# A top-2 expert layer with a shared expert: every expert over every token, or 23 tiles of routed rows fetched through DRAM

## The chip, the cores and the metric

The kernel runs on one core of a Trainium2 chip. The time is the device time of one execution in microseconds. The core has a matrix engine (TensorE, PE in the profile; PEld is its weight load), a vector engine (DVE), a scalar engine (ACT), a general engine (POOL) and a queue engine (SP) that issues most DMA transfers.

## The reference

A stack of four layers works on x of 4 x 256 tokens with 256 features (1024 tokens in all), each layer an attention over a context of 1601 rows and a feed-forward part, both with a layer norm ahead and a residual sum behind. The change is in the last feed-forward part and reaches into the attention ahead of it (16 heads of 128, 4 key heads, over the same context). Cut to what matters:

```python
# E = 8 experts of width 128, top 2; a shared expert of width 512
x = x + attention_3(layernorm(x), ctx)
h = layernorm(x).reshape(1024, 256)
probs = softmax(h @ w_gate)
topk_w, topk_ids = top_k(probs, 2)
topk_w = topk_w / sum(topk_w)
combine = sum(topk_w * one_hot(topk_ids, 8))
act = silu(g) * u      for g, u = split(einsum('th,ehf->etf', h, w_gate_up))
eo = einsum('eti,eih->eth', act, w_down)
routed = einsum('te,eth->th', combine, eo)
shared = (silu(g) * u for g, u = split(h @ w_sh_gate_up)) @ w_sh_down
x = x + routed + shared
```

All numbers are f32.

## The kernel before

The tokens lie in eight tiles X[0] to X[7] of 128 tokens by 256 features; a batch b of the four is the pair X[2b], X[2b+1].

**The last feed-forward part** (`shared_moe`, L1905 to L1957) starts from a transposed norm of all tokens (`layernorm`, halves of 512 tokens). `router` (L187) makes all probabilities, `top2` the two choices, and `comb` holds one weight per token and expert. Then a loop runs over the eight experts and, last, the shared expert; inside it over the two halves. Per half of an expert it makes gate and up products for 512 tokens (L1942), `gated` (L1745, L1746) makes silu times up, and four down products (L1948) come back with 128 tokens on the partitions. Each is added to X with the expert's weight (L1955), whatever that weight is: an expert works on all 1024 tokens, also on those that did not choose it. The shared expert has four such gate and up parts per half and sums four products per tile; its sums go by `residual` (L181) and the tiles are stored (L1953). TensorE, ScalarE and VectorE are ordered here by the scheduler.

**The attention ahead of it** (`gqa`, L1001) is laid out by hand in slots. Sixteen units (batch and key head) take 16 slots each; slot t has phases "first", "early", "mid", "late", "last", "values", "pe", "post", and `at(slot, phase, f)` puts a step there. The scores of a slot go to two of three PSUM tiles (L1235); VectorE takes their maxima (L1243), ScalarE the exponentials (L1244), which also frees the tile; POOL scales them (L1284), VectorE transposes blocks (L1289), and TensorE makes the value products (L1315) and the output products (L1328), which `residual` adds to X. The engines TensorE, ScalarE, VectorE and POOL keep the written order; SP is ordered by the scheduler.

**The same routing elsewhere.** The first layer's feed-forward part already works on routed rows: `send_to_experts` (L586) ranks each token within its expert and scatters rows to the DRAM table XS (L727), and `sparse_moe` (L738) fetches tiles of 128 rows from it (L817), the first eight at fixed rows and fifteen more at rows held in registers (L805). The third layer's `capacity_moe` (L1749) scatters (L1845), fetches (L1853), stores results (L1888) and gathers them back per token (L1899). Each expert has room for 1024 rows in XS, so 2048 routed rows of eight experts need at most 8 + 15 = 23 tiles of 128.

Of the kernel before, what the change touches and what calls it, by code (L numbers as in the profile page):

```python
# [12 lines left out]
F32 = mybir.dt.float32  # L13
I32 = mybir.dt.int32
# [38 lines left out]
def kernel(ctx: ExitStack, tc: tile.TileContext, A, out: bass.AP):  # L53
# [683 lines left out]

    def sparse_moe(r, k, XS, XD, tabs):  # L738
        ET = mybir.EngineType
        NT = E + MORE  # L740
        with (
# [18 lines left out]
            for f in r["last"]:  # L760
                f()

            ps = ps_acc()
            nc.tensor.matmul(ps[:, 0:E], k["ones"], r["cum"], start=True, stop=True)
            cnt = small([P, E], "d_cnt", 1)
            nc.vector.tensor_copy(cnt, ps[:, 0:E])
            over = small([P, E, E - 1], "d_over", 1)
            nc.vector.tensor_tensor(
                over, cnt.unsqueeze(2).to_broadcast([P, E, E - 1]),
                k["step"].unsqueeze(1).to_broadcast([P, E, E - 1]), ALU.is_gt,  # L770
            )
            nc.vector.tensor_reduce(cnt, over, AX.X, ALU.add)
            upto = small([P, E], "d_upto", 1)
            t8 = small([P, E, E], "d_t8", 1)
            nc.vector.tensor_tensor(t8, k["tri8"], cnt.unsqueeze(1).to_broadcast([P, E, E]), ALU.mult)
            nc.vector.tensor_reduce(upto, t8, AX.X, ALU.add)
            oh = one.tile([P, MORE, E], F32, tag="d_oh", name="d_oh")
            g = one.tile([P, MORE, E], F32, tag="d_g", name="d_g")
            wide = [P, MORE, E]
            more = k["more"].unsqueeze(2).to_broadcast(wide)  # L780
            nc.vector.tensor_tensor(oh, more, upto.unsqueeze(1).to_broadcast(wide), ALU.is_ge)
            ex = small([P, MORE], "d_ex", 1)
            nc.vector.tensor_reduce(ex, oh, AX.X, ALU.add)
            nc.vector.tensor_tensor(
                oh, k["expert"].unsqueeze(1).to_broadcast(wide), ex.unsqueeze(2).to_broadcast(wide), ALU.is_equal
            )

            nc.vector.tensor_tensor(cnt, cnt, upto, ALU.subtract)
            nc.vector.scalar_tensor_tensor(cnt, cnt, float(P), k["first"], ALU.mult, ALU.add)
            nc.vector.scalar_tensor_tensor(  # L790
                g, more, float(P), cnt.unsqueeze(1).to_broadcast(wide), ALU.mult, ALU.add
            )
            nc.vector.tensor_tensor(g, g, oh, ALU.mult)
            row = small([P, MORE], "d_row", 1)
            nc.vector.tensor_reduce(row, g, AX.X, ALU.add)
            none = small([P, MORE], "d_none", 1)
            nc.vector.tensor_scalar(none, ex, E - 0.5, float(E * ROOM), ALU.is_gt, ALU.mult)
            nc.vector.tensor_tensor(row, row, none, ALU.add)
            nc.vector.tensor_scalar(ex, ex, E - 1.0, 4096.0, ALU.min, ALU.mult)
            ix = one.tile([P, 2, MORE], I32, tag="d_ix", name="d_ix")  # L800
            nc.vector.tensor_copy(ix[:, 0, :], row)
            nc.vector.tensor_copy(ix[:, 1, :], ex)
# [198 lines left out]
    def gqa(xT, key, tabs=None, early=None):  # L1001
# [12 lines left out]
        with (  # L1014
# [324 lines left out]

            weights(0)  # L1340
# [564 lines left out]
    def shared_moe(xT):  # L1905
        with (
            tc.tile_pool(name="l3f", bufs=2) as pool,
            tc.tile_pool(name="l3f1", bufs=1) as one,
        ):
            wg = one.tile([P, NC_, E], F32, tag="wg", name="wg")  # L1910
            nc.sync.dma_start(wg, A["l3f_wg"])
            ws = []
            for k in range(2):
                w = wslot()
                nc.sync.dma_start(w[:, 0:3072].rearrange("p (e f) -> p e f", e=4), A["l3f_w"][:, k * 4 : (k + 1) * 4, :])
                ws += [w[:, i * 768 : (i + 1) * 768] for i in range(4)]
            shw = wslot()
            nc.sync.dma_start(shw[:, 0:3072], A["l3f_sw"])
            probs = router(one, xT, wg)
            m1, m2, comb = top2(one, probs)  # L1920
            nc.vector.tensor_tensor(m1, m1, m2, ALU.add)
            nc.vector.reciprocal(m1, m1)
            nc.vector.tensor_tensor(comb, comb, bc(m1, E), ALU.mult)

            parts = []
            for e in range(E):
                gu = ws[e][:, 0:512].rearrange("p (c f) -> p c f", c=2)
                parts.append(([(gu[:, :, 0:I3], gu[:, :, I3:])], [ws[e][:, 512:768]], e))
            sgu = shw[:, 0:2048].rearrange("p (c f) -> p c f", c=2)
            parts.append((  # L1930
                [(sgu[:, :, i * P : (i + 1) * P], sgu[:, :, ISH + i * P : ISH + (i + 1) * P]) for i in range(4)],
                [shw[:, 2048 + i * D : 2048 + (i + 1) * D] for i in range(4)],
                None,
            ))
            for gus, downs, e in parts:
                for hf in range(2):
                    acts = pool.tile([P, len(gus), 512], F32, tag=f"act{len(gus)}", name="acts")
                    for i, (wgt, wup) in enumerate(gus):
                        pg, pu = ps_acc(), ps_acc()
                        for ps, wt in ((pg, wgt), (pu, wup)):  # L1940
                            for c in range(NC_):
                                nc.tensor.matmul(ps, wt[:, c, :], xT[hf][:, c, :], start=(c == 0), stop=(c == NC_ - 1))  # L1942
                        gated(pool, acts[:, i, :], pg, pu)
                    for t in range(4):
                        j = hf * 4 + t
                        ps = ps_tr()
                        for i, wd in enumerate(downs):
                            nc.tensor.matmul(  # L1948
                                ps[:, :D], acts[:, i, t * P : (t + 1) * P], wd, start=(i == 0), stop=(i == len(downs) - 1)
                            )  # L1950
                        if e is None:
                            residual(j, ps[:, :D])
                            nc.sync.dma_start(out[j * P : (j + 1) * P, :], X[j])  # L1953
                        else:
                            nc.vector.scalar_tensor_tensor(  # L1955
                                X[j], ps[:, :D], comb[:, j, e : e + 1], X[j], ALU.mult, ALU.add
                            )  # L1957
# [11 lines left out]
    with tc.tile_pool(name="sort", bufs=1) as sortp:  # L1969
        k = sort_constants(sortp)  # L1970
        with rings(0, x=0, s1=2, kv=2, tr=2, acc=2):
            r = topk_attention(lambda: send_to_experts(sortp, k, XS), KD, VD)
        with rings(0, x=0, tr=3, acc=5):
            sparse_moe(r, k, XS, XD, tabs)
# [96 lines left out]
```

## Time and profile before

| what | value |
|---|---|
| median of three runs | 3896.47 us (3893.48 to 3897.65) |
| the profiled execution | 3896.89 us, of which the span of the profile is 3895.1 us |
| TensorE busy | 3656.7 us, 94% of the span |
| VectorE, ScalarE, POOL busy | 2612.1, 1677.2, 1278.0 us |
| mean granted TensorE clock | 0.971 of full speed |

The span is the time from the first to the last instruction of the profiled execution; the time of the execution is 1.8 us longer. Instructions are named by engine, line, operation and by the tiles they write and read. A matmul of f32 data is listed as two. "Idle before" is the time in which an engine waited ahead of an instruction, with what ended the wait.

### The profile page before, as it was taken

The numbers are of one execution on the slowest core, as the hardware profiler recorded it, in microseconds if no ns is written. First come the engines' busy times: TensorE is split into PE (matmuls) and PEld (weight loads), VectorE is DVE, ScalarE is ACT, GpSimd is POOL, SyncE is SP. The second block draws the span as 40 slices with busy tenths as digits, with TensorE's granted clock in tenths as the row PEclk, the third lists the DMA queues.
The fourth block names the chain that finished last, engine by engine and source line by source line (L and its number), as shares of the span: only waits on it lengthen the run. The fifth ranks groups of instructions, "written<-read, shape, count | busy, mean of one in ns | idle before, by whom it ended". The sixth has DMA issues, their size and how long they took to land.

```text
span 3895.1 us, 62649 instructions
## 1 busy us (share of the span) xinstructions
PE 3656.7 (94%) x23428; PEld 2176.8 (56%) x23428; DVE 2612.1 (67%) x5037; ACT 1677.2 (43%) x4898; POOL 1278.0 (33%) x2046
## 2 busy tenths in 40 slices
PE   8887969999999999999899999987999999999999
PEld 4557945555555555555445454563455565555555
DVE  7884857777777777777566565436777766666653
ACT  4443635444444444454134444513344444454421
POOL 2332535444544544443300101013333333333310
PEclk9987979999999999999999999988999999999999
DMA  7326342222222221210200000033111011111010
GB/s 236 101 66 236 79 148 62 64 81 57 55 66 62 75 66 54 65 51 1 72 1 18 6 13 1 1 138 114 51 44 58 28 40 50 34 41 41 7 49 11
DMA packets 165553, 238.22 MB, mean 61 GB/s; under 512 B 20333, under 2 KB 127745, under 8 KB 161665
## 3 DMA queue, kind: packets, MB, share of 16 engines
q1 hardware_dynamic: 160401, 226.96, 18.8%
q0 software_dynamic: 4848, 7.25, 1.0%
q8 instruction: 186, 3.05, 0.3%
q14 instruction: 118, 0.97, 0.1%
HBM read 194.28 MB, written 39.88 MB: 60 GB/s over the span
## 4 chain that ended last, share of the span: by engine, by line
PE 65%; DVE 18%; POOL 7%; issue 5%; ACT 3%; DMA 2%; SPq 0%; DVEq 0%; POOLq 0%; ACTq 0%
PE acc L1315 15%; PE sc L1235 13%; PE tr L1104 5%; PE sc L1608 4%; DVE PT L1289 4%; PE sc L1562 3%; PE tr L1178 3%; PE acc L1629 3%; POOL pe L1284 3%; PE acc L877 2%; PE acc L1942 2%; PE tr L1517 2%; PE tr L1328 2%; POOL t L1151 2%; DVE ms L1243 2%
## 5 line engine op out<-in xcount | busy, mean ns | idle before, releaser
L1244 ACT ACTIVATE pe<-sc,ms 128x480 f32<-128x480 f32 (+1 forms) x1024 | 644.1, 632 | 942.1 <-DVE ms L1243 923.7
L1315 PE MATMUL acc<-PT,V 128*128 128x256 f32 (+1 forms) x3584 | 897.7, 391 | 7.7 <-ACT OT L1322 7.2
L1235 PE MATMUL sc<-KT,QT 128*32 128x480 f32 (+5 forms) x8192 | 888.0, 535 | 14.0 <-ACT pe L1244 6.2
L1284 POOL TENSOR_SCALAR pe<-pe,fac 128x480 f32<-128x480 f32 (+1 forms) x1024 | 654.9, 659 | 636.5 <-ACT pe L1244 304.9
L1315 PEld LDWEIGHTS acc<-PT,V 128*128 128x128 f32 (+1 forms) x3584 | 643.0, 190 | 350.7 <-issue 181.9
L1243 DVE TENSOR_REDUCE ms<-sc 128x1 f32<-128x480 f32 (+1 forms) x1024 | 607.9, 615 | 170.3 <-PE sc L1235 145.5
L1289 DVE STREAM_TRANSPOSE PT<-pe 128x1920 f32<-128x1920 f32 (+1 forms) x256 | 519.5, 2030 | 0.0
L122 POOL TENSOR_TENSOR rs<-rsq_t,mhalf 128x2 f32<-128x2 f32 (+2 forms) x248 | 159.9, 645 | 880.8 <-DVE rsq_t L121 821.5
L1235 PEld LDWEIGHTS sc<-KT,QT 128*32 128x32 f32 x8192 | 218.8, 109 | 408.6 <-issue 308.6
L1104 PE MATMUL tr<-w,cx 128*128 128x256 f32 (+1 forms) x1264 | 303.3, 382 | 1.3 <-ACT nk L1120 1.3
L1614 ACT ACTIVATE pt<-sc 128x1024 f32<-128x1024 f32 (+1 forms) x224 | 214.1, 960 | 201.1 <-PE sc L1608 192.8
L1568 DVE TENSOR_REDUCE mx<-sc 128x2 f32<-128x1024 f32 (+1 forms) x192 | 207.2, 1089 | 114.6 <-PE sc L1562 65.3
L1608 PE MATMUL sc<-QT,KT 32*128 32x256 f32 (+1 forms) x1664 | 235.8, 405 | 21.2 <-DVE mx L1568 14.5
L1104 PEld LDWEIGHTS tr<-w,cx 128*128 128x128 f32 (+1 forms) x1264 | 227.0, 187 | 31.6 <-ACT nk L1120 2.0
L1562 PE MATMUL sc<-KT,QT 32*128 32x512 f32 (+2 forms) x1024 | 229.1, 553 | 0.7 <-DVE mx L1568 0.6
L1244 ACT ACTIVATION_READ_ACCUMULATOR pe<-sc,ms 128x1 f32 x1024 | 199.9, 195 | 0.0
L1608 PEld LDWEIGHTS sc<-QT,KT 32*128 32x128 f32 (+1 forms) x1664 | 136.7, 183 | 79.0 <-DVE mx L1568 51.2
L122 POOL TENSOR_TENSOR rsq<-rsq_t,mhalf 128x4 f32<-128x4 f32 x64 | 64.9, 1014 | 324.4 <-DVE rsq_t L121 324.4
L1112 ACT ACTIVATE sq<-tr 128x128 f32<-128x128 f32 (+1 forms) x348 | 97.1, 279 | 170.7 <-PE tr L1104 164.2
L121 DVE TENSOR_SCALAR rsq_t<-ss 128x2 f32<-128x2 f32 (+2 forms) x248 | 46.4, 188 | 177.2 <-ACT sq L1112 139.8
L1178 PE MATMUL tr<-w,xlnT 128*128 128x512 f32 x256 | 125.1, 612 | 4.4 <-DMA w<-in_l1a_wkv 4.1
L1562 PEld LDWEIGHTS sc<-KT,QT 32*128 32x128 f32 x1024 | 84.3, 190 | 76.6 <-issue 41.8
(373 smaller groups left out, 4864.2 us busy)
## 6 DMA issues: line engine op xcount, KB each, us to landing
cx<-in_ctxT SPq DMA_DIRECT2D x144, 256.0 KB, 3.1
tab<-rope SPq DMA_DIRECT2D x112, 256.0 KB, 2.7
w<-in_l0f_w SPq DMA_DIRECT2D x8, 2048.0 KB, 14.4
ctxT<-in_ctxT SPq DMA_DIRECT2D x7, 1601.0 KB, 7.3
w<-in_l2f_w SPq DMA_DIRECT2D x8, 1088.0 KB, 18.1
w<-in_l1a_wq SPq DMA_DIRECT2D x16, 512.0 KB, 5.9
wo<-in_l1a_wo SPq DMA_DIRECT2D x16, 512.0 KB, 7.7
w<-in_l3a_wq SPq DMA_DIRECT2D x16, 512.0 KB, 5.9
```

Of the source, the lines that this page charges most:

```text
L122: nc.gpsimd.tensor_tensor(dst, t[:n, :k], mhalf[:n, :k], ALU.pow)
L1104: nc.tensor.matmul(v["ps"][:n, i, :], lhs, st["wkv"][:, c, :], start=(c == 0), stop=(c == NC_ - 1))
L1178: nc.tensor.matmul(v["ps"], xtok(xT, b * 2 + tt, c), state[u]["wq"][:, c, :], start=(c == 0), stop=(c == NC_ - 1))
L1235: nc.tensor.matmul(sc[32 * r : 32 * r + 32, 0 : lens[r]], st["QT"][:, tt, o : o + 32], st["KT"][:, r, 0 : lens[r]], start=True, stop=True,)
L1243: nc.vector.tensor_reduce(top, sc, AX.X, ALU.max, negate=True)
L1244: nc.scalar.activation(w, sc, AF.Exp, bias=top, accum_out=s)
L1284: nc.gpsimd.tensor_scalar(w, w, v["fac"][:, g * 4 + a : g * 4 + a + 1], 1.0, ALU.mult, ALU.mult)
L1289: nc.vector.transpose(state[steps[i]][:, :, g * P : (g + 1) * P].rearrange("p k (a t) -> p a k t", a=4), pes[g].rearrange("p a (k i) -> p ...
L1315: nc.tensor.matmul(v["ps"][:, 0 : 2 * P], V[:n, k, :], PT[:n, k, :], start=(k == 0), stop=(k == nch - 1))
L1562: nc.tensor.matmul(st[:, j, :n], QT[r, g, tt * P : (tt + 1) * P], KT[r, g, o : o + n], start=True, stop=True)
L1608: nc.tensor.matmul(st[:n, j, q, :], KT[r, g, o : o + n], QT[r, :], start=True, stop=True)
L1614: nc.scalar.activation(pt[:n, 2 * hp : 2 * hp + 2, :m], st[:n, :, :m], AF.Exp)
```

## The change

`shared_moe` no longer runs every expert over every token.

- `send_to_shared` makes norm, router, both choices, weights and ranks of one batch in small steps. For batches 0 to 2, `others` puts these steps into free slots of the attention, from slot 4(16b + 15) + 13 on, with four scatters of 128 rows each (two tiles, two choices) to XS, one per slot. Table constants and the shared expert's weights are made or loaded ahead of the attention.
- After the attention, `shared_moe` writes its order by hand for TensorE, ScalarE and VectorE. The first part of the shared expert's first half (`up(0, 0)`) stands ahead of the last batch's norm and routing; `up(0, 1)`, `up(0, 2)`, `up(0, 3)` and the sums `down(0)` stand between and behind its steps.
- `more_tiles` (taken out of `sparse_moe`, where its steps stay the same) finds from the counts which expert and row each of the fifteen further tiles has. A register with the row is loaded on SP for each fetch, and one with the weight's column on TensorE for each tile, tile by tile.
- Each of the 23 tiles is fetched, transposed (`turn`), multiplied with gate and up weights together (`first`), gated, transposed back (`back`), multiplied with the down weights (`second`) and stored to the DRAM table OQ.
- Then come `up(1, 0)` to `up(1, 3)`. `collect(j)` gathers two rows per token from OQ, adds them with their weights to X[j] and stores the tile: tiles 0 to 3 ahead of the sums `down(1)`, 4 to 7 behind them.

The diff, cut to its core:

```diff
-    def shared_moe(xT):
...
-            for gus, downs, e in parts:
-                for hf in range(2):
...
+        def others(at, done):
+            for b in range(B - 1):
+                t = done(b)
+                p = batch(b)
+                for i, phase, name in (
+                    (0, "early", "stats"), (0, "late", "scale"), (1, "pe", "turn"), (2, "early", "turned"),
+                    (2, "pe", "logits"), (3, "early", "exps"), (4, "late", "probs"), (5, "late", "first"),
+                    (6, "late", "second"), (7, "late", "count"), (8, "pe", "ranks"), (9, "early", "rows"),
+                ):
+                    at(t + i, phase, p[name])
+                for q in range(4):
+                    at(t + 9 + q, "late", lambda p=p, q=q: p["send"](q // 2, q % 2))
...
+            rest = up(0, 0)
+            for name in ("stats", "scale", "turn", "turned", "logits", "exps", "probs", "first", "second", "count"):
+                last[name]()
+            rest()
+            rest = up(0, 1)
+            last["ranks"]()
+            last["rows"]()
+            for q in range(4):
+                last["send"](q // 2, q % 2)
+            rest()
+            up(0, 2)()
+            ix, _, _, less = more_tiles(one, k, r["cum"], float(WIDE3))
...
+            def fetch(t):
+                x = pool.tile([P, D], F32, tag="xs", name="xs", bufs=8)
+                if t < E:
+                    nc.sync.dma_start(x, XS[t * ROOM : t * ROOM + P, 0:D])
+                else:
+                    nc.sync.dma_start(x, XS[bass.ds(register(ET.SP, 0, t - E, E * ROOM), P), 0:D])
...
+            for t in range(E):
+                fetch(t)
...
+            up(0, 3)()
+            down(0)
+
+            def turn(t):
+                v = tiles[t]
+                if t >= E:
+                    v["at"] = register(ET.PE, 1, t - E, (E - 1) * WIDE3)
+                tr = ps_tr()
+                for c in range(NC_):
+                    nc.tensor.transpose(tr[:, c * P : (c + 1) * P], v["x"][:, c * P : (c + 1) * P], ident)
+                v["xT"] = pool.tile([P, NC_, P], F32, tag="xsT", name="xsT", bufs=3)
+                nc.vector.tensor_copy(v["xT"], tr[:, 0:D].rearrange("p (c t) -> p c t", c=NC_))
...
+            def second(t):
+                v = tiles[t]
+                ps = ps_acc()
+                nc.tensor.matmul(ps[:, 0:D], v["aT"], part(t, 4 * I3, 4 * I3 + D), start=True, stop=True)
+                y = pool.tile([P, D], F32, tag="y", name="y", bufs=4)
+                nc.scalar.copy(y, ps[:, 0:D])
+                nc.sync.dma_start(OQ[t * P : (t + 1) * P, :], y)
+
+            for t in range(NT + 3):
+                for f, i in ((turn, t), (first, t - 1), (back, t - 2), (second, t - 3)):
+                    if 0 <= i < NT:
+                        f(i)
+                if E <= t + 5 < NT:
+                    fetch(t + 5)
+            for i in range(4):
+                up(1, i)()
...
+            def collect(j):
+
+                b, i = divmod(j, 2)
+                y = one.tile([P, 2, D], F32, tag=f"g{j}", name=f"g{j}")
+                for c in range(2):
+                    nc.gpsimd.indirect_dma_start(
+                        y[:, c], None, OQ[:, :], bass.IndirectOffsetOnAxis(ap=iq[:, b, c, i : i + 1], axis=0)
+                    )
+                for c in range(2):
+                    nc.vector.scalar_tensor_tensor(X[j], y[:, c], r["w"][:, b, c, i : i + 1], X[j], ALU.mult, ALU.add)
+                nc.sync.dma_start(out[j * P : (j + 1) * P, :], X[j])
+
+            for j in range(4):
+                collect(j)
+            down(1)
+            for j in range(4, NJ):
+                collect(j)
...
-    with rings(3):
-        shared_moe(layernorm())
+    with tc.tile_pool(name="sort3", bufs=1) as sortp:
+        shw = sortp.tile([P, 3072], F32, tag="shw", name="shw")
+        nc.sync.dma_start(shw, A["l3f_sw"])
+        with rings(0, sc0=1, sc1=1, sc2=1, tr=4, acc=1):
+            xT = layernorm()
+            k = sort_constants(sortp)
+            r, batch, others = send_to_shared(sortp, k, XS)
+            gqa(xT, "l3a", early=(EARLY, KD, VD), others=others)
+        with rings(0, x=0, tr=3, acc=5):
+            shared_moe(r, k, shw, batch(B - 1), XS, OQ)
```

## The prediction

> **What bounds the kernel now.** I read the page, then the chain of waits in order of time, then the windows by stage.
>
> ```profile
> span 3895.1 us, 62649 instructions
> PE 3656.7 (94%) x23428; PEld 2176.8 (56%) x23428; DVE 2612.1 (67%) x5037; ACT 1677.2 (43%) x4898; POOL 1278.0 (33%) x2046
> ```
>
> TensorE is busy throughout, so work taken from it should count. The end of the chain (start, time, engine, tile, line) is the changed stage:
>
> ```profile
> 3749.61 1.74 PE tr L1328 x8
> ...
> 3808.66 2.57 PE acc L1942 x6
> 3814.09 2.58 PE acc L1942 x6
> ...
> 3852.05 12.02 PE acc L1942 x28
> 3864.06 6.91 PE tr L1948 x32
> ```
>
> L1328 is attention's last product; it ends at 3751.4, and the stage takes 3895.1 - 3751.4 = 143.7 us. Call 3751.4 zero. An f32 product is listed as two matmuls (passes). One period of 5.43 us (3814.09 - 3808.66) is half an expert: eight passes of 512 columns and eight of 256. The last two lines give 0.43 us a pass of 512 and 0.216 us a pass of 256.
>
> The windows (length; busy PE, PEld, DVE, ACT, POOL; granted clock, DMA share, GB/s) compare the stages:
>
> ```profile
> 2700.00:2800.00 100.00, 95.25 (x649) 49.64 (x643) 71.42 (x135) 39.28 (x119) 31.36 (x51) 1.00 0.12 39
> 3500.00:3600.00 100.00, 98.35 (x658) 58.16 (x654) 66.05 (x137) 48.77 (x171) 36.94 (x60) 1.00 0.16 44
> 3755.00:3762.00 7.00, 6.92 (x32) 6.52 (x33) 1.39 (x4) 0.58 (x1) 0.00 (x0) 0.50 1.01 421
> 3800.00:3850.00 50.00, 50.00 (x149) 27.38 (x149) 23.12 (x47) 5.37 (x9) 0.00 (x0) 1.00 0.00 0
> ```
>
> The routed stage is TensorE alone at full clock; POOL and the queues are idle. Attention ahead of it has TensorE at 95 to 98% and VectorE at 66 to 71%: work moved there finds little room on TensorE.
>
> **Removed.** Routed products: 16 periods x 5.43 = 86.9 us. Norm and router between 3751.4 and 3761.6: 10.2 us, part of it at half clock.
>
> **Added on TensorE: the tile loop.** A tile costs two transposes, two products of 256 columns, a transpose and one more product. Six passes x 0.216 = 1.30; a transpose of 128 columns has a pitch of 0.11 us (the two of L855 start 0.22 us ahead of the next product), so 0.33. That is 1.63 us, and 23 tiles take 37.5 us. Beside it per tile lie VectorE 0.42 (copy, L857) + 0.29 (128x128 product, L1660) and ScalarE 0.28 + 0.28 + 0.37 (L1112, L1887's form) = 0.93, both shorter and one to two tiles behind, so hidden. Filling and draining the pipeline adds about 2.
>
> **Register loads.** Fifteen tiles load one register each on TensorE's queue and one on SP's. The old expert stage loads fifteen in one instruction (L805):
>
> ```profile
> L805 PEldq TENSOR_LOAD <-d_ix x1: 4428/4428/4428, 306.6 to 306.6; - x1
> L805 SPq TENSOR_LOAD <-d_ix x1: 1892/1892/1892, 348.8 to 348.8; - x1
> ```
>
> Divided, one is 0.13 (SP) to 0.30 us (TensorE, with weights streaming in). The Trainium skill (DMA: Bandwidth & Descriptors, "Latency and other measured facts") speaks against loading singly: it gives a floor of about 600 ns to a load, to be spread by unrolling four. By the row the fifteen cost 2 to 4.5 us of the queue, by the rule 9. Either lies behind matmuls already sent, if the queue runs ahead: a tile's last input is ready some 0.4 us into its 1.63 us, so about 0.9 us is covered. No row shows a load among running matmuls; bounds are 0 and the whole 4.43 each (52 us after cover). I take 2 us in all, nearest the divided row, and keep up to 9. The address arithmetic on TensorE's queue (46 ns each at L896) left its eight passes at 1.89 us there, so nothing. SP has a load, a fetch (0.34, L817) and a store (0.32, L1888) per tile, 0.8 to 1.3 us against 1.63: eight buffers and stores one tile late keep it off the path, unless its load took over 1 us. The gate's table load (1.28 us, ScalarE) is in both kernels and lies beside the routing.
>
> **Added: the last batch's routing.** The old expert stage has the same chain: from its last sum (290.4) to the rows (302.2) 11.8 us, in small vector steps of 0.17 every 0.21. Here the first shared product (0.5 to 3.9) delays the transposes by 1 us and one gate product sits in the chain: rows at about 13.4. Four scatters follow on POOL:
>
> ```profile
> 2574.99 0.96 POOL L1845 DMA_INDIRECT xd<-nat,ix  x1 [0.30 <-issue]
> 2576.26 0.96 POOL L1845 DMA_INDIRECT xd<-nat,ix  x1 [0.30 <-issue]
> ...
> 2578.67 3.65 SPq L1853 DMA_DIRECT2D xs<-xd  x8
> ```
>
> One each 1.27 us; SP fetches 2.4 us after the last begins. So issues at 13.5 to 17.3, fetch at 20, first tile by 22.5 (2.1 us to landing). Beside it TensorE does four shared parts (13.8), the routing's own passes (2) and the first four sums (6.9). It waits twice: about 1.1 us for the ranks, and for the fourth shared part's gate, because VectorE does the tables first: 4.1 us as at L766 to L802, then twelve more steps, 2.8 us, so the gate at 23.2 while that product ended at 18.4 and the six passes that need no gate at 19.7. That is 3.6 us idle; the remaining 26 passes end at 28.9.
>
> Does the clock fall? The rows around 3733:
>
> ```profile
> 3714.12 2.00 PE L1315 MATMUL acc<-PT,V 128*128 128x256 f32 x8
> ...
> 3733.91 3.40 PE L1315 MATMUL acc<-PT,V 128*128 128x256 f32 x8
> ```
>
> After 1.85 us without a matmul eight passes took 3.40 instead of 2.00 us, and the slow stretch lasted about 5. The Trainium skill (TensorE: Matmul & The Clock Gate, "Part 1: The HAM clock gate") asks for at least one idle window of about 3.4 us first. By the row the 1.1 us wait is nearly enough too and both together cost 3; by the rule only the long one, 1.7 at most. I take 2: loop from 30.9. The tiles have landed by then.
>
> **The end.** Loop 37.5 + 2 + 2, to 72.4. Copy 0.4 and the store's landing 1.7 (L1888), with gaps: 74.8. Then sixteen gathers on POOL, where capacity_moe's eight ran every 1.25 us and landed in 2.8 (L1899): last issued at 74.8 + 15 x 1.25 = 93.6, landed 96.4, weighted sum 0.48 each: 97. From the last sum to the end of the span the old kernel took 3895.1 - 3892.1 = 3.0: 100. TensorE's other shared half ends at 72.4 + 13.7 + 0.9 + 6.9 = 93.9, so the gathers are late next, by 3 us. The stage gains 143.7 - 100 = 43.7.
>
> **Moved into attention (three batches).** TensorE each: four transposes 0.45, eight narrow passes and four rank passes at about 0.13 = 1.6; together 2.1, x3 = 6.3 us with next to no slack (9.6 if the passes cost the 0.21 of L193 at half clock). VectorE: about 7 us each over twelve slots, in order ahead of score maxima that release TensorE's score banks; a slot of 3.6 to 4.5 us has 1.2 to 1.5 free. Nothing to 7 us a batch can show; I take 5 in all, since most steps come after the maxima. POOL: twelve scatters of 1.26 us, one a slot, each waiting for the one before; they precede L1284's scalings, whose transposes follow two slots later, so 0 (12 x 1.26 = 15 us were that slack gone). At the start thirteen table and fill instructions (2 us) stand on POOL ahead of the first rsqrt, and SP issues 1.5 MB of shared weights and the gate ahead of attention's weights (0.8 us of issue, 3.7 us at 421 GB/s); the first weights wait about 3 us for their norm now, which covers most: 1 us, at most 4. Sum 12.3. The routed weights come at the end while TensorE does shared work (3 MB, 7.5 us): covered until 22.
>
> **Sum.** -43.7 + 12.3 = -31.4. The profiled execution took 3896.9 (1.8 outside its span), the median 3896.5: 3865.
>
> **Rivals.**
> - *The moves are free* (chance 0.17): attention absorbs the vector steps, the clock stays up, loads hide. Then 5 + 1 + 2 + 2 us fall away: 3855. For it: VectorE is 29 to 34% idle there. Against: 95% busy TensorE with waits on maxima.
> - *VectorE stalls attention* (0.13): all 7 us of each batch show, 21 instead of 5: 3881. For it: ScalarE waits for maxima all through (L1244 on L1243). Against: maxima mostly have 2 us of bank slack.
> - *Slower: single register loads stop TensorE* (0.07). In the tile loop each load waits with the queue empty at the full 4.43 us; 15 x (4.43 - 0.9) = 53 less the 2 counted: 3916. Above about 3.1 us a load, the gain is gone. For it: the only TensorE load traced cost that. Against: it read fifteen values, and SP's took 1.89.
> - That the tiles are not made is excluded: their count is fixed at 23 whatever is routed, 2944 rows against 8192.
>
> **Numbers.** The forecast has 0.63. A difference under 0.2% (7.8 us) is about what a measurement here cannot tell from none. Faster: 0.61 + 0.17 + 0.08 = 0.86; same: 0.02 + 0.05 = 0.07; slower 0.07. The range reaches down to the free moves with the gathers hidden too (3) and TensorE's 6.3 in its gaps, 3846, and up to stalled attention (3881) with loads at the rule's 9 us and a start of 4, 3891.
>
> **What would show it.** Right: 1.6 us between tiles from the eighth on as before it, attention's last product 10 to 15 us later, sixteen gathers back to back at the end with TensorE done. Wrong: TensorE idle at each load; tiles waiting for fetches behind stores on SP; attention longer by over 20 us; or routing so late that the first tile waits.

## The result and the profile after

The changed kernel took 3858.86 us (median of six runs, 3857.5 to 3860.84) against 3895.88 us before (six runs beside it, 3892.45 to 3897.65). The ratio is 0.9905, 95% interval 0.9894 to 0.9915: 37 us faster. The forecast was 3865 us, with faster at 0.86; the time lies in the range and 6 us under the forecast.

The first two lines of the page after (span; busy time, share and instructions of each engine):

```profile
span 3856.3 us, 63026 instructions
PE 3603.5 (93%) x23397; PEld 2157.0 (56%) x23397; DVE 2611.3 (68%) x5142; ACT 1688.0 (44%) x4956; POOL 1310.3 (34%) x2091
```

TensorE's busy time fell by 53 us, but only 38.8 us of it came out of the span: TensorE is no longer what ends the kernel. The chain of waits says what does (start, time, engine, tile, line):

```profile
3756.44 1.74 PE tr L1335 x8
...
3758.68 3.70 PE acc L2104 x8
...
3780.45 5.89 PE tr L2113 x26
...
3819.01 0.87 PE acc L2194 x4
...
3820.64 0.87 PE acc L2194 x4
...
3825.04 1.73 PE acc L2104 x4
...
3827.94 0.99 POOL g L2230
...
3847.20 3.18 DMA g<-oq,g_ix
```

L1335 is attention's last product. The residual sum behind it starts at 3758.20, which I call zero as the prediction did for before (3751.37 there). L2104 is a shared part, L2113 the shared sums, L2194 a tile's gate and up product: 3820.64 - 3819.01 = 1.63 us a tile. From 3827.94 on the chain is gathers. The stage ends at 98.1 us from zero; before it took 143.7.

The windows (length; busy PE, PEld, DVE, ACT, POOL; granted clock, DMA share, GB/s):

```profile
2700.00:2800.00 100.00, 95.06 (x648) 48.86 (x646) 71.02 (x135) 39.79 (x122) 32.30 (x53) 1.00 0.12 39
3500.00:3600.00 100.00, 97.91 (x653) 59.82 (x645) 70.08 (x168) 47.30 (x166) 37.18 (x57) 1.00 0.17 49
3758.00:3765.00 7.00, 5.76 (x23) 3.16 (x23) 2.20 (x8) 0.58 (x1) 0.71 (x1) 1.00 0.83 314
3795.00:3820.00 25.00, 25.00 (x140) 21.11 (x139) 10.80 (x31) 12.17 (x46) 0.00 (x0) 1.00 0.42 129
```

Attention's stretches hardly changed; behind zero the clock is full where before it was half, and the tile loop fills TensorE, though each tile has a register load.

### The profile page after: what moved, and what is told of

Its sections match the earlier page's. It is cut to its first block, busy times and chain, and to the rows that moved or that the text cites. A ratio compares the mean times of both kernels' runs of the same rounds, so it can differ in the third digit from the quotient of the medians.

```text
span 3856.3 us, 63026 instructions
## 1 busy us (share of the span) xinstructions
PE 3603.5 (93%) x23397; PEld 2157.0 (56%) x23397; DVE 2611.3 (68%) x5142; ACT 1688.0 (44%) x4956; POOL 1310.3 (34%) x2091
## 4 chain that ended last, share of the span: by engine, by line
PE 64%; DVE 18%; POOL 7%; issue 5%; ACT 3%; DMA 3%; SPq 1%; POOLq 0%; DVEq 0%; ACTq 0%
PE acc L1322 15%; PE sc L1242 13%; PE tr L1111 5%; PE sc L1618 4%; DVE PT L1296 4%; PE sc L1572 3%; PE tr L1185 3%; PE acc L1639 3%; POOL pe L1291 3%; PE acc L884 2%; PE tr L1527 2%; PE tr L1335 2%; POOL t L1158 2%; DVE ms L1250 2%; ACT pe L1251 2%
## 5 line engine op out<-in xcount | busy, mean ns | idle before, releaser
L1250 DVE TENSOR_REDUCE ms<-sc 128x1 f32<-128x480 f32 (+1 forms) x1024 | 607.5, 615 | 173.3 <-PE sc L1242 147.2
```

Of the source, the lines that this page charges most:

```text
L1250: nc.vector.tensor_reduce(top, sc, AX.X, ALU.max, negate=True)
```

## The experiments

All times of the table come from one profiled execution each, the medians from all runs. "Attention" runs from the first score maximum (L1250, before L1243) of the third unit to zero. It leaves out the stages ahead, which no edit touches and which came out up to 10 us apart between executions (2771.1 us in one_load, 2781.2 in part_behind). The kernel before took 3894.8 to 3897.4 us in the median beside the groups of runs. The other columns count from zero. Before: attention 975.0 us, end 143.7.

| kernel | median us | ratio to before, 95% | attention | first tile | last gather begins | end |
|---|---|---|---|---|---|---|
| after | 3858.9 | 0.9905 (0.9894 to 0.9915) | 983.1 | 28.0 | 89.0 | 98.1 |
| again | 3861.0 | 0.9910 (0.9893 to 0.9926) | 983.1 | 28.0 | 88.7 | 97.7 |
| stats_late | 3854.9 | 0.9894 (0.9879 to 0.9909) | 980.0 | 29.6 | 90.7 | 101.6 |
| tables_late | 3860.5 | 0.9908 (0.9893 to 0.9923) | 983.2 | 25.5 | 86.5 | 97.5 |
| sums_late | 3863.6 | 0.9918 (0.9904 to 0.9931) | 983.2 | 22.2 | 84.9 | 102.4 |
| part_behind | 3871.2 | 0.9929 (0.9915 to 0.9942) | 983.2 | 34.2 | 95.2 | 106.2 |
| route_after | 3901.9 | 1.0012 (1.0003 to 1.0021) | 976.7 | 74.6 | 135.6 | 146.6 |
| one_load | 3868.4 | 0.9921 (0.9907 to 0.9934) | 987.3 | 29.7 | 90.7 | 101.6 |
| loads6 | 3866.1 | 0.9919 (0.9906 to 0.9933) | 987.3 | 29.7 | 93.7 | 104.2 |
| best | 3855.6 | 0.9893 (0.9878 to 0.9908) | 980.0 | 22.1 | 82.9 | 98.9 |
| copied | 3860.0 | 0.9907 (0.9891 to 0.9924) | 983.2 | 28.0 | 89.0 | 98.1 |
| two_late | 3854.2 | 0.9894 (0.9878 to 0.9911) | 979.9 | 25.5 | 86.5 | 95.6 |
| three | 3852.1 | 0.9884 (0.9867 to 0.9900) | 980.0 | 25.5 | 86.5 | 95.6 |

**What the moves into attention are worth (route_after).**

```diff
-                if b == B - 1:
+                if True:
                     tc.declare_no_dep(ins, group="rows3", reason="no two tokens have the same row of an expert")
...
-            gqa(xT, "l3a", early=(EARLY, KD, VD), others=others)
+            gqa(xT, "l3a", early=(EARLY, KD, VD))
...
+            for b in range(B - 1):
+                p = batch(b)
+                for name in ("stats", "scale", "turn", "turned", "logits", "exps", "probs", "first", "second", "count", "ranks", "rows"):
+                    p[name]()
+                for q in range(4):
+                    p["send"](q // 2, q % 2)
+            last = batch(B - 1)
             rest = up(0, 0)
```

> The edit: the routing of batches 0 to 2 is not put into attention's slots but made, batch by batch, between attention and the first shared part. Theory A (in attention it costs 2.8 us a batch, behind it the whole chain shows): attention ends 8 us earlier, but each batch takes about 11.8 us from its norm to its rows, the scatters going beside the next batch: 35 us, so about 27 us slower than the changed kernel, 3886. Theory B (the batches' chains overlap on VectorE, whose own steps are 7 us a batch): 21 - 8 = 13 us slower, 3872. Theory C (TensorE idle for this long also lowers its clock for the parts that follow): 2 to 4 us on top of either.

The scatters of all batches are here declared independent of each other, as only the last batch's were. The kernel was slower than expected by every theory, and no faster than the kernel before: 3901.9 us against 3897.4 beside it (1.9 us of it belong to the wait of the last point of this part). Attention came out 6.4 us shorter, but the first tile 46.6 us later. POOL in the timeline:

```profile
3766.84 0.96 POOL L2055 DMA_INDIRECT xs<-nat,row  x1 [0.30 <-issue]
3767.83 0.73 POOL L122 TENSOR_TENSOR rstd<-rsq_t,mhalf 128x2 f32<-128x2 f32 x1
3779.12 1.04 POOL L2055 DMA_INDIRECT xs<-nat,row  x1 [10.56 <-DVE row L2052]
```

and VectorE's waits (us in total, times, longest):

```profile
DVE nat L1963 <- POOL rstd L122: 13.9, 3, 4.6
```

The power step of the next batch's norm is queued on POOL behind four scatters of 1.27 us: 4.6 us more a batch. The first scatters of the second and third batch are 16.16 us apart (3779.12 and 3795.28), not 11.8. The granted clock stood at half for 41 us of it. So the tile loop by itself gains nothing over the dense experts: without the slots of attention the routing takes back the 49 us by which the tiles are shorter than the products that they replace (86.9 less 37.5).

**Where the moves cost attention (stats_late).**

```diff
-                    (0, "early", "stats"), (0, "late", "scale"), (1, "pe", "turn"), (2, "early", "turned"),
-                    (2, "pe", "logits"), (3, "early", "exps"), (4, "late", "probs"), (5, "late", "first"),
-                    (6, "late", "second"), (7, "late", "count"), (8, "pe", "ranks"), (9, "early", "rows"),
+                    (0, "late", "stats"), (1, "late", "scale"), (2, "pe", "turn"), (3, "early", "turned"),
+                    (3, "pe", "logits"), (4, "early", "exps"), (5, "late", "probs"), (6, "late", "first"),
+                    (7, "late", "second"), (8, "late", "count"), (9, "pe", "ranks"), (10, "early", "rows"),
...
-                    at(t + 9 + q, "late", lambda p=p, q=q: p["send"](q // 2, q % 2))
+                    at(t + 10 + q, "late", lambda p=p, q=q: p["send"](q // 2, q % 2))
```

> The edit: in attention each batch's norm statistics move from the "early" phase of their slot to "late", behind the score maxima, and every later step moves one slot on. In the changed kernel's trace each batch costs attention 2.9 us: the TensorE passes 1.63 (0.44 + 0.82 + 0.37) and 1.27 at one place, where the statistics stand ahead of L1276 to L1279, for which TensorE waits (idle 1.53 instead of 0.27 us). Theory A (a stall at one place): 3 x 1.27 = 3.8 us less than the changed kernel, about 3855 against 3858.9, attention's last product 3.8 us earlier. Theory B (VectorE's added load costs this wherever its steps stand): no change, 3859. Theory C (the next place stalls: the scaling, now a slot later, holds up maxima): a gain under 1.5 us.

After's timeline, VectorE at the first of the three places, then TensorE:

```profile
2956.79 0.38 DVE L1954 BATCH_NORM_STATS2 bnst<-x 128x6 f32<-128x256 f32 x1
2957.20 0.18 DVE L1955 BATCH_NORM_AGGREGATE bnmv<-bnst 128x2 f32<-128x6 f32 x1
...
2959.09 0.28 DVE L1279 TENSOR_TENSOR cf<-cf,top 8x128 f32<-8x128 f32 x1
```

```profile
2959.52 0.20 PE L1283 MATMUL tr<-ident,cf 8*128 8x8 f32 x1 [1.53 <-DVE cf L1279]
```

The five statistics steps precede the four steps that end in L1279, and TensorE's small transpose waits for those. In stats_late that row reads

```profile
2954.86 0.20 PE L1283 MATMUL tr<-ident,cf 8*128 8x8 f32 x1 [0.27 <-DVE cf L1279]
```

The wait of 1.26 us is gone and attention is 3.1 us shorter, with as many vector steps as ever. That speaks for A against B: it was a place, not a load. 0.7 us of the 3.8 stayed, so the later slots cost something too. Attention repeats well enough to show this: 983.1 to 983.2 us in the six traces that have after's order there and no further slow stretch of the clock, 979.9 to 980.0 in the four with this edit. The median fell by 4 us, with intervals that overlap, and this execution lost 3.5 us again behind zero; the next point and the last of this part say how.

**TensorE's wait for the gate, and the clock (tables_late).** The block that makes g_ix (L2154 to L2169) moves from ahead of up(0, 3) to behind it:

```diff
+            up(0, 3)()
             n = 4 * B
             ew, fr = (r[q].rearrange("p b c i -> p (b c i)") for q in ("ex", "at"))
...
             nc.vector.tensor_tensor(iq.rearrange("p b c i -> p (b c i)"), line, far, ALU.add)
-            up(0, 3)()
             down(0)
```

> The edit: the twelve VectorE steps for the gather table move behind the gate of the fourth shared part up(0, 3). In the changed kernel TensorE is idle 2.79 us ahead of the 26 passes of the shared sums that need this gate. Theory A (these steps delay the gate, and the tile loop and all behind it start with the sums): 2.8 us less than the changed kernel, about 3856; the loop's first transposes 2.8 us earlier. Theory B (the loop is bound by its fetch): no change, the first transpose waits for its row tile instead. Theory C (the moved steps hold up the residual sums that release the three banks of the sums): a gain under 1 us.

The sums in the timelines of after, of stats_late and of two_late, which has this edit too:

```profile
3780.45 5.88 PE L2113 MATMUL tr<-shw,acts 128*128 128x256 f32 x26 [2.79 <-DVE acts L1756]
```

```profile
3773.91 7.57 PE L2113 MATMUL tr<-shw,acts 128*128 128x256 f32 x26 [2.79 <-DVE acts L1756]
```

```profile
3774.38 5.88 PE L2113 MATMUL tr<-shw,acts 128*128 128x256 f32 x26 [0.34 <-DVE acts L1756]
```

The edit does what A said: the wait falls by 2.45 us, and first tile and last gather come 2.5 us earlier. Yet tables_late itself ended only 0.6 us earlier, and its median did not fall; the last point of this part has the reason. In two_late the whole 2.5 us shows at the end.

The three rows also settle the clock term. After the same wait of 2.79 us the same 26 passes took 5.88 us in one execution and 7.57 in another. In stats_late the window (granted clock third from the end) reads

```profile
3775.40:3778.80 3.40, 3.40 (x10) 2.74 (x9) 0.43 (x1) 0.00 (x0) 0.00 (x0) 0.53 0.35 96
```

Half clock for one stretch of 3.41 us. Of the eight executions with this wait five had such a stretch behind it (stats_late, part_behind, one_load, loads6, route_after), three had not (after, again, copied). The clock records of the traces show what parts them. The slow stretches of one execution start on a grid of 3.41 us, and this grid lies elsewhere in each execution. The window of the grid that holds most of the wait, in after and in stats_late:

```profile
3778.66:3782.07 3.41, 1.62 (x8) 1.44 (x9) 1.99 (x8) 0.00 (x0) 0.00 (x0) 1.00 0.82 231
3771.79:3775.20 3.41, 1.29 (x6) 1.16 (x7) 2.25 (x10) 0.00 (x0) 0.00 (x0) 1.00 0.72 192
```

TensorE was idle for 1.79 us of the one and 2.12 of the other. In all five executions with a slow stretch 2.12 to 2.79 us of the wait lay in one window, in the three others 1.79 to 1.87. The wait is the same; where it falls in the grid goes with the clock.

The same is seen in attention: one_load and loads6 have after's attention, 4.1 us longer, because each of the three places that stats_late mends was followed by such a stretch. In one_load:

```profile
2955.61 0.20 PE L1283 MATMUL tr<-ident,cf 8*128 8x8 f32 x1 [1.52 <-DVE cf L1279]
2955.74 2.98 PE L1242 MATMUL sc<-KT,QT 128*32 128x416 f32 x16
```

where after needs 1.91 us for the sixteen passes. For these waits of 1.5 us the grid gives no clean line: with about 45% of the window idle a slow stretch followed in one_load and loads6, and none in part_behind. A short wait of TensorE therefore costs its own length, and 1.3 to 1.7 us more in some executions.

**The first part ahead of the norm (part_behind).**

```diff
-            rest = up(0, 0)
-            for name in ("stats", "scale", "turn", "turned", "logits", "exps", "probs", "first", "second", "count"):
+            for name in ("stats", "scale", "turn", "turned", "logits"):
+                last[name]()
+            rest = up(0, 0)
+            for name in ("exps", "probs", "first", "second", "count"):
                 last[name]()
```

> The edit: the first shared part up(0, 0) moves from ahead of the last batch's norm to behind its gate product, so TensorE has nothing while the norm is made. Theory A (work that covered the norm is now uncovered): TensorE's 3.5 us show, about 3862. Theory B (what sets the loop's start is VectorE: the tables stand ahead of the gate for which TensorE now waits 2.8 us): the routing starts 1 us earlier because its transposes no longer wait behind the product, TensorE's later work goes into the 2.8 us, and the time falls by up to 1 us, about 3858.

Both theories failed: the median rose by 12 us, and the first tile came 6.2 us later. TensorE in the timeline:

```profile
3770.26 9.34 PE L2104 MATMUL acc<-xT,shw 128*128 128x512 f32 x16
3779.43 0.29 PE L2040 MATMUL tr<-r_both,k_tri 128*128 128x16 f32 x2
```

The sixteen passes now stand together ahead of the rank product, whose inputs VectorE had ready at 3774.5, so it comes 4.9 us late in TensorE's queue. And TensorE, idle for 2.74 us while the norm was made, ran some of these passes at half clock (9.34 us; sixteen at 0.43 are 6.9). The wait of 2.79 us for the gate was still there, since the gate waits for VectorE, whose rows came later; behind it came another slow stretch of 1.7 us. Of the median's 12 us the trace explains half: this execution lost 8.1 us behind zero, 1.9 of them with the wait of the last point, and was 6.1 us longer in the stages ahead of attention, which the edit does not touch. So the order of the changed kernel does two things at once: it covers the norm, and it puts one part, not two, ahead of the ranks.

**Register loads (one_load, loads6).** The edits:

```diff
-                    ix[0:1, which, i : i + 1], engines=[engine], min_val=0, max_val=top,
+                    ix[0:1, which, :], engines=[engine], min_val=0, max_val=top,
...
-                )[1][0]
+                )[1]
+            rows = register(ET.SP, 0, 0, E * ROOM)
...
+            cols = register(ET.PE, 1, 0, (E - 1) * WIDE3)
```

> The edit: the fifteen rows are loaded into registers by one instruction on SP and the fifteen columns by one on TensorE ahead of the loop, in place of one each per tile. Theory A (the single loads of 0.30 us on TensorE's queue lie behind running matmuls): nothing gained in the loop, 1.63 us a tile as now; the one load takes 1.9 us on SP and up to 4.4 us on TensorE's queue ahead of the first transpose, so 0 to 4 us slower than the changed kernel, 3859 to 3863. Theory B (each single load stops TensorE for its 0.30 us): tiles from the eighth on 0.3 us shorter, 4.5 us less in all, about 3856 if the one load is covered.

```diff
-                    v["at"] = register(ET.PE, 1, t - E, (E - 1) * WIDE3)
+                    for _ in range(6):
+                        v["at"] = register(ET.PE, 1, t - E, (E - 1) * WIDE3)
```

> The edit: each of the fifteen register loads on TensorE's queue is made six times, 1.8 us of the queue a tile in place of 0.30. Theory A (about 0.9 us a tile is covered, the prediction's number): each of the fifteen tiles takes 0.9 us longer, 13.5 us in all, about 3872. Theory B (the queue runs a whole tile ahead, 1.6 us of cover): 0.2 us a tile, 3 us in all, about 3862. Theory C (nothing is covered, and the single load already stands in the 1.63 us): 1.5 us a tile, 22.5 us in all, about 3881.

The load of each tile in after (durations in ns: least, median, greatest):

```profile
L2142 SPq TENSOR_LOAD <-d_ix x15: 273/278/455, 3782.1 to 3808.2; - x15
L2142 PEldq TENSOR_LOAD <-d_ix x15: 299/302/318, 3796.8 to 3819.1; - x15
```

With one load for all fifteen the tiles stayed at 1.63 us: B of one_load is out. In one_load it took 3.58 us on TensorE's queue and cost nothing either: the first tile came at 29.7 us, as in stats_late, which has the same slow stretch and no such load. Three of one_load's five runs lay 7 us above the other two; its profile is of one of those two, so what the three lost stays open.

loads6 did not do what it was made for. The kernel that ran still has one load a tile, with five more semaphore steps ahead of it, 0.15 us each, 0.75 us of queue a tile; the load itself took 0.47 us in the median. The last six full tiles then took 1.73 to 1.74 us instead of 1.63. So the queue has room for the one load and for some 0.7 us more, then it shows: near the 0.9 us that the prediction took for the cover. None of the three theories was put to its test.

**What ends the kernel (sums_late, best).** The edits move down(0), or half of it, behind up(1, 3); best has the edits of stats_late and tables_late besides.

```diff
             up(0, 3)()
-            down(0)
...
             for i in range(4):
                 up(1, i)()
+            down(0)
```

> The edit: the shared sums down(0), 32 passes, move from ahead of the tile loop to behind it and behind up(1, 3). Loop and gathers then start when the first row tile has landed, about 22.2 us after attention's last residual instead of 27.9, so 5.6 us earlier. Theory A (the gathers are what binds the end, by 5 us): they land 5.6 us earlier and the time falls by nearly that, about 3853.5. Theory B (TensorE takes over): its last product comes at 87.5 - 5.6 + 7.0 = 88.9 us, the residual sum at 89.3, and the eight weighted sums that VectorE's order puts behind it take 3.8: 93.1, as late as the last sum now (92.7), so no gain, about 3859. Theory C (TensorE idle for some 3.8 us ahead of the loop lowers its clock): 2 to 3 us slower than now, with passes of the first tiles at twice their time.

> The edit: three things together: statistics behind the maxima in attention, table steps behind the fourth gate, and of the shared sums down(0) two tiles ahead of the loop and two behind up(1, 3). Theory A: attention 3.8 us shorter; the loop starts when its first tile has landed, at 22.4 us instead of 27.9; TensorE's last product then comes at 87.5 - 5.5 + 3.5 = 85.5 us, just ahead of the last gather at 86.7, so the last sum comes 5.5 us earlier: 9.3 us less in all, about 3849.6. Theory B (TensorE and the weighted sums behind its residuals bind the end): half of the 5.5 shows, about 3852. Theory C (attention's vector steps stall elsewhere): 3853.5.

In sums_late the loop starts at 22.2 us and the last gather begins 4.1 us earlier, but the end comes 4.3 us later. TensorE waits 4.0 us for the first tile, with a slow stretch behind it, and at the end it is TensorE that is late, as B said, but with its last product at 95.6 us and not at 88.9. Part of this is the slow stretch, part a long wait of VectorE for TensorE:

```profile
3834.17 0.42 DVE L181 TENSOR_TENSOR x<-tr,x 128x256 f32<-128x256 f32 x1 [0.96 <-PE tr L2113]
3841.48 0.42 DVE L181 TENSOR_TENSOR x<-tr,x 128x256 f32<-128x256 f32 x1 [6.89 <-remote]
```

"Remote" is the profile's word for a releaser that it doesn't know. best has the same wait (6.8 us) and two_late, below, has not. So what either order of the sums would give without this wait is not shown: best ended at 98.9 us with it, two_late at 95.6 without.

**The 7 us (again, copied, two_late, three).** In tables_late VectorE stands as long at the second half's sums:

```profile
3841.10 0.42 DVE L181 TENSOR_TENSOR x<-tr,x 128x256 f32<-128x256 f32 x1
3848.67 1.09 DVE L181 TENSOR_TENSOR x<-tr,x 128x256 f32<-128x256 f32 x3 [7.15 <-remote]
```

All eight of the first experiments show such a wait of 6.1 to 7.2 us, once each, beside the gathers; after does not. Four more kernels were run to tell whether it belongs to the order of work:

> The changed kernel once more, unaltered. In its first trace VectorE ran the four residual sums of down(1) without a break; in the eight other kernels' traces it stood 6 to 7 us still after the first residual sum that met the gathers, with TensorE's product long ready. Theory A (the stall belongs to this order of work, and the first trace was the exception): the trace shows it, the last weighted sum comes some 4 us later after the gathers, and attention and loop repeat to 0.1 us a batch and a tile. Theory B (only the edits bring it): no stall. The median should repeat 3859 within 2 us.

```diff
-                    residual(h * 4 + t, ps[:, :D])
+                    if h:
+                        s = one.tile([P, D], F32, tag=f"s{t}", name=f"s{t}")
+                        nc.scalar.copy(s, ps[:, :D])
+                        residual(h * 4 + t, s)
+                    else:
+                        residual(h * 4 + t, ps[:, :D])
```

> The edit: for the second half alone, ScalarE copies each shared sum from PSUM to SBUF and VectorE adds the copy, so VectorE reads no PSUM while the gathers run. Theory A (VectorE's PSUM reading sums are what stands still beside the gathers): no stall, the last weighted sum right after the last gather's landing, and the span ends with POOL's drain, 8.1 us after the last gather begins, plus 0.9; about 3857. Theory B (any VectorE instruction can stand still there): the 7 us stall is there again, on an addition of a copy; 3858 to 3860.

two_late is stats_late and tables_late together; three is two_late with the copies.

> The edit: statistics behind the maxima in attention, and the table steps behind the fourth gate; down(0) stays ahead of the loop. Theory A (both gains of the single edits add, 3.1 in attention and 2.5 at the loop's start, and the stall beside the gathers takes some of the second back): 4 to 5 us less than the changed kernel, about 3854. Theory B (the stall takes all of the second): as with the statistics alone, 3855.

> The edit: two_late with the copies of copied as well. Theory A (without the stall the gathers' drain sets the end): attention 3.1 less, loop 2.5 earlier and gathers with it, so 5.6 us less than the changed kernel where that had no stall, about 3853. Theory B (the stall stays): as two_late, 3854 to 3855.

None of the four shows it. It is not a matter of the order: again is after unaltered, and two_late has the orders of two kernels that had it. copied tells nothing about its cause. What VectorE waited for is TensorE's signal, in both kinds of trace. In after the semaphore records of the last three tiles' sums come at 84.04, 85.77 and 87.50 us from zero, 1.73 us apart, the time of a tile's eight passes. In tables_late they come at 90.03, 90.12 and 90.21. Products that were made only then could not follow at 0.09 us, so at least the last two tiles' were done earlier, and the signals were late. TensorE's closing drain lasts as much longer, first in after, then in tables_late:

```profile
L2358 PEldq DRAIN  x2: 13/1050/2088, 3843.6 to 3855.8; - x2
L2358 PEldq DRAIN  x2: 13/3643/7273, 3841.6 to 3855.6; - x2
```

Why the signals were late is open. Two more things part the eight traces from the others, and no run here separates them. The eight were taken on two chips, and the four without the wait later on a third. And many semaphore records beside the gathers are missing in the eight (25,547 to 25,636 records in the whole trace, 26,089 to 26,102 in the five without the wait), so the wait may come with the recording and not with the kernel. It makes the last weighted sum some 4.5 us later (7.8 us from the last gather's beginning in tables_late, 3.3 in after) and the end 1.9 us (11.0 instead of 9.1).

Without it the end is exactly regular. In two_late the last gather begins at 3841.12 and its data are summed at

```profile
3844.41 0.48 DVE L2234 SCALAR_TENSOR_TENSOR x<-g,w,x 128x256 f32<-128x256 f32 x1 [1.18 <-DMA g<-oq,g_ix]
```

yet the span ends at 3850.2. In every execution POOL's closing drain ends 8.1 to 8.3 us after the last gather begins, and the span 0.8 us after that if nothing else is later: 89.0 + 8.25 + 0.8 = 98.1 in after, 86.5 + 8.25 + 0.8 = 95.6 in two_late. In after:

```profile
L2358 POOLq DRAIN  x3: 51/113/15963, 3839.5 to 3856.0; - x3
```

The longest of the three, 15.96 us, lasts from 3839.5 to 3855.5; the last store was issued at 3851.0, and the stores landed 2.2 to 2.6 us after their issue, so by 3853.6. That the drain waits for the gathers is read from the constant distance, in thirteen executions whose ends differ; what it does after their data have landed no record shows.

two_late and three beat both kernels: 3854.2 and 3852.1 us. In the group that they ran in, the changed kernel took 3858.6 to 3863.0 and three 3847.4 to 3854.6, which do not meet; the intervals of the ratios to before still overlap. What their traces explain is 3.2 us in attention and 2.5 behind zero.

## Why the prediction was right, and what was mis-sized

The likeliest case came in: the stage is bounded by the gathers with TensorE done (its last product ended at 3845.7, 4.7 us ahead of the last gather's landing), tiles take 1.63 us on both sides of the eighth, and the moves cost attention more than nothing and less than the gain. The profiled span fell by 38.8 us where the sum said 31.4. One sign named ahead did not come: attention's last product came 6.8 us later, not 10 to 15. By its steps:

- *Moved into attention, 12.3 us.* Zero moved by 6.8 us. Attention itself grew by 8.1 us (983.1 - 975.0, with one slow stretch of the clock in each; route_after, without the moves, had two and 976.7), and the stages ahead were 1.3 us shorter in this execution. The start's 1 us can't be told from that scatter.
  - TensorE, predicted 6.3: the passes displaced the score maxima by 0.44 + 0.82 + 0.37 = 1.63 us a batch, 4.9. The narrow passes were priced too high.
  - VectorE, predicted 5: 1.27 us a batch, 3.8. Together that is 8.7, a little over the 8.1 measured. The size was fair but not the picture. I looked for stalls ahead of the score maxima; the stall sat ahead of L1276 to L1279, because the statistics were put into "early" before the softmax tail was, in the one slot in four that has this tail there.
  - POOL, predicted 0: no wait at the scatters shows.
- *The last batch's routing.* Rows at 13.1 us (13.4 predicted), fetch at 19.8 (20). The row that answers to the scatters shown of before:

```profile
3775.54 0.96 POOL L2055 DMA_INDIRECT xs<-nat,row  x1 [0.30 <-issue]
```

  and they are 1.27 us apart as there.
- *Idle TensorE, 3.6 predicted for the gate, 1.1 for the ranks:* 2.79 and 0.36.
- *Clock, 2 us:* nothing in this execution, 1.7 in five of eight; that it was nothing is luck. I had set the row of before against the rule; both answers left out where the wait falls in the grid. The slow stretch of before, which I took for about 5 us, is 3.41 us of half clock as well (3734.34 to 3737.75). In after even the place that slowed before went by at full speed:

```profile
3742.28 0.22 PE L1283 MATMUL tr<-ident,cf 8*128 8x8 f32 x1 [1.85 <-DVE cf L1279]
3742.43 1.99 PE L1322 MATMUL acc<-PT,V 128*128 128x256 f32 x8
```

  The Trainium skill (TensorE: Matmul & The Clock Gate, "Part 1: The HAM clock gate") says that the activity window of 3413 ns is free-running; the slow stretches here are indeed 3.41 us long or a multiple of it, and the same wait of 2.79 us lay with 1.79 us in one window of after and with 2.12 in one of stats_late. But its "idle window" as a condition is too strict for these traces: waits of 1.5 to 2.8 us, well under a window, were enough at times. By the rule read strictly this term is 0; read by the row it is a chance of 1.7.
- *Register loads, 2 us:* nothing. 0.30 us each on TensorE's queue is the upper divided row, half of the skill's floor of 600 ns (DMA: Bandwidth & Descriptors, "Latency and other measured facts"), and the cover of 0.9 us took it. The slower rival needed over 3.1 us a load and is out.
- *Loop.* Predicted from 30.9 to 72.4, measured from 28.0 to 66.8. 23 x 1.63 = 37.5, and filling and draining 1.4 instead of 2.
- *The end, the term that was too small.* From the last gather's beginning I counted 2.8 to land, 0.6 to sum and 3.0 to the end of the span: 6.4. It is 9.1, because POOL's drain, which the kernel before didn't have to wait for (there it was over at 3759.1), outlasts the stores. The step that failed is to carry over from before the 3.0 us between the last sum and the end of the span: it is 5.3 here (3850.95 to 3856.3).

So attention was overpriced by 5.5 us, clock and loads by 4, and the end underpriced by 2.7. The remaining difference is small terms of either sign. Of the rivals, free moves (3855) was nearer in time than in mechanism: attention did pay.

## What to carry to other kernels

Work moved into the slots of a full stage costs its passes on the bounding engine (4.9 us here) and nearly as much again by where it is queued (3.8, of which 3.1 came back): put it behind the steps that the bounding engine waits for in that slot, not ahead of them. Ask of a sparse version first whether its routing can be hidden: here the tiles saved 49 us of products (86.9 less 37.5), and the same tiles with the routing in the open were no faster than the dense experts. And where a program ends with gathers from GpSimd, count to the end of its drain, 9 us from the last gather's beginning here, not to the last sum.

## What the runs showed of the hardware

- The granted clock falls to half for 3.41 us, or a multiple, after waits of TensorE as short as 1.5 us, in some executions and not in others with the same code; 1.3 to 1.7 us each. The stretches of one execution lie on one grid of 3.41 us; behind the wait of 2.79 us the clock fell where 2.12 us or more of it lay in one window of the grid (five executions), and not where it was 1.87 us or less (three).
- A single register load takes 0.28 us on SP and 0.30 on TensorE's queue, and is hidden beside 1.63 us of matmuls; with 0.75 us of semaphore steps more a tile took 1.73 us.
- GpSimd's closing drain ended 8.1 to 8.3 us after its last gather began, in all thirteen executions of the changed kernel and its variants.
- Beside GpSimd's gathers VectorE waited 6.1 to 7.2 us for TensorE's signal in eight of these thirteen. In tables_late three signals came 0.09 us apart whose products take 1.73 us each. The cause is open.
- The stages ahead of the change differ by up to 10 us between executions (2771.1 to 2781.2 us), though no edit touches them. Differences in the span of two profiles under that size are read stage by stage, not from the spans.
